# Scattering 80 instead of 72 edge columns one by one into a dense adjacency matrix

## The chip, the core and the metric

The kernel runs on one core of a Trainium2 chip. The metric is the device time of one execution in microseconds (us); lower is better. The core's engines are called as the profile calls them: PE (matmuls; PEld is its weight load), DVE (vector), ACT (activations), POOL (GpSimd, which here issues the indirect DMAs) and SP (which issues most of the plain DMAs).

## The reference, cut to what matters

One transformer layer: `x = x + attn(layernorm(x))`, then `x = x + ffn(layernorm(x))`, with x of shape (4, 1024, 256). The feed-forward part is a mixture of 8 experts, two for each token; it fills most of the time and isn't touched. In the attention part there is a sparse sum over a list of 32768 edges (row, column, value), and the change lies in how that sum is prepared:

```python
q = enc @ wq                                   # enc: attention output of batch 0 + dense
k = enc @ wk
scores = jnp.einsum('bid,bjd->bij', q, k) / jnp.sqrt(jnp.float32(WQK_DIM))
data = scores[0]                               # 1024 x 1024
contrib = adj_vals * data[adj_rows, adj_cols]
A_raw = jax.ops.segment_sum(contrib, adj_rows, num_segments=n)
alpha = jax.nn.softmax(A_raw)                  # one weight per row; used for every token
```

Rows and columns are drawn up to 2047 while n is 1024. An edge whose row is 1024 or more is dropped by the segment sum; a column of 1024 or more is clamped to 1023. So about a quarter of the edges have a row below 1024 and a column below 1023 (about 64 in each of 128 groups of 256 edges), and another quarter have the last column.

## The kernel before

**Edges.** The 32768 edges lie as 256 columns on 128 partitions. `edge_keys` (L203) marks the edges with a row below 1024 and a column below 1023 and makes three sort keys of each. `pick` (L251) takes the eight largest of each partition's keys with DVE's `max` and strikes them out; `picks` (L715) repeats that over groups of eight, so that after eleven groups the valid edges of a partition stand in order in `CC` = 88 packed columns. Edges of the last column go another way (`edge_last`, L368): one-hot tiles `ohl` on DVE and matmuls, 16 columns at a time, between the softmax work.

**A.** The sum becomes dense: A is a 1024 x 1024 matrix of edge values in DRAM, and `A_raw` comes from a matmul of A with k and a product with q. A exists as `PL` = 2 planes, `a_d[0]` and `a_d[1]`, zeroed at the start. `edge_pack` (L263) makes a cell number and a value for some of the packed columns with six small DVE operations, and `scatter` (L275) writes them: for each column one indirect DMA on POOL's queue, 128 single values, column i into plane i % 2. All 128 partitions take part; where a partition has no i-th valid edge, the cell number is out of bounds and nothing is written. Every eighth scatter (`REST` = 8) has an added dependence on the one before it.

**The rest.** Columns 0 to `CD` - 1 are scattered that way. The columns from `CD` to 87 hold few valid edges, and `edge_rest` (L291) puts these together into one column: it counts them (`full`, `nrest`), finds with a small matmul (L303) where each partition's rest begins, makes a one-hot tile `ohrest` of 128 x w on DVE (L310), with w = `CC - CD`, and moves the bytes of the edges with w small matmuls (L327) to `prest`. From there a handful of DVE operations make one cell and one value per partition, and column `CD` is scattered last (L342).

**Order of the work.** The groups of eight are picked in the steps `todo = {0: range(4, 6), 1: range(6, 9), 2: range(9, CC // 8)}` of the loop over the head pairs (L994), the earlier ones ahead of it; `picks` calls `edge_pack` for that part of its columns that lies below `CD`. The scheduler of the framework then orders each engine's instructions by dependences and priorities; each engine runs its own list in that order. On POOL's list the scatters stand one behind another, and each waits until the scatter eight places before it (on the same of eight completion semaphores) has landed.

**What needs A.** `counted` (L1071) reads both planes back, 1024 rows in eight steps c: `av` is the part of plane 0, `ac` that of plane 1, 512 KB each, read by SP's queue. DVE makes `nz` (which entries aren't zero, L1079) of each, PE sums these with sixteen tiny matmuls for each c (L1083), and DVE adds `ac` to `av` (L1086). There are three buffers for `nz` and two for `ac`. Plane counts are compared with the edge counts per row (`one_lo` and `one_hi` of `edge_hots`, L344, with the 88 small matmuls of L1110); a row in which two edges fell on one cell is `bad`, and its edges are done one by one (`direct`, L407). Between the scatters and this use PE has other work: the products `po` with the convolution band (L1047, L1057) and the q and k products `pqk` (L1093, L1095).

Of the kernel before, what the change touches and what calls it, by code (L numbers as in the profile page):

```python
# [11 lines left out]
ALU = mybir.AluOpType  # L12
# [4 lines left out]
P = 128  # L17
# [8 lines left out]
E = 32768  # L26
EC = E // P
CC = 88
CD = 72
EG = 8  # L30
DQ = 64
PL = 2
# [16 lines left out]
def tile_kernel(  # L49
# [137 lines left out]
    packed = [ed.tile([P, CC], F32, name=f"packed{i}") for i in range(3)]  # L187
    cell = ed.tile([P, CD + 1], I32, name="cell")
    pval = ed.tile([P, CD + 1], F32, name="pval")
    most = ed.tile([P, 1], F32, name="most")  # L190
# [84 lines left out]
    def scatter(cols):  # L275
        for i in cols:
            ins = nc.gpsimd.indirect_dma_start(  # L277
                out=a_d[i % PL],
                out_offset=bass.IndirectOffsetOnAxis(ap=cell[:, i : i + 1], axis=0),
                in_=pval[:, i : i + 1], in_offset=None,  # L280
                bounds_check=N * N - 1, oob_is_err=False,
            ).ins
            if i and i % REST == 0:
                tc.add_manual_dep(
                    ins, scattered[-1].name,
                    mybir.DependencyInfo(mybir.DependencyClass.Sync, mybir.DependencyReason.DATA),
                    reason="rest",
                )
            scattered.append(ins)

    def edge_rest(et, ps):  # L291


        w = CC - CD
        def some(name, dt=F32, w=w):
            return et.tile([P, w], dt, name=name, bufs=1)

        full, n, base = some("full"), some("nrest", w=1), some("base", w=1)
        first = packed[0][:, CD:]
        nc.vector.tensor_scalar(full, first, 0.0, None, ALU.not_equal)  # L300
        nc.vector.tensor_reduce(n, full, AX.X, ALU.add)
        pt = ps.tile([P, 512], F32, tag="ps", name="prest")
        mm(pt[:, 0:1], lhsT=low, rhs=n, start=True, stop=True)  # L303
        nc.vector.tensor_scalar(base, pt[:, 0:1], 512.0, None, ALU.add)
        to, tob = some("to"), some("tob", BF16)
        nc.vector.tensor_scalar(to, iota[:, 0:w], base, None, ALU.add)
        nc.vector.scalar_tensor_tensor(to, full, -512.0, to, ALU.mult, ALU.add)
        nc.vector.tensor_scalar(tob, to, 255.0, None, ALU.min)
        oh = et.tile([P, P, w], BF16, tag="ohl", name="ohrest")
        nc.vector.tensor_tensor(  # L310
            oh, tob.unsqueeze(1).to_broadcast([P, P, w]), iota_x, ALU.is_equal
        )

        bi = et.tile([P, 7, w], I32, name="restb", bufs=1)
        k = 0
        for s3, masks in zip(packed, ((255, 255, 15), (255, 255), (255, 255))):
            for j, mask in enumerate(masks):
                nc.vector.tensor_scalar(
                    bi[:, k], s3[:, CD:].bitcast(I32), 8 * j, mask,
                    ALU.logical_shift_right, ALU.bitwise_and,  # L320
                )
                k += 1
        by = et.tile([P, 8, w], BF16, name="rest8", bufs=1)
        nc.vector.tensor_copy(by[:, 0:7], bi)
        nc.vector.tensor_copy(by[:, 7], full)
        for i in range(w):
            mm(pt[:, 8:16], lhsT=oh[:, :, i], rhs=by[:, :, i], start=(i == 0), stop=(i == w - 1))  # L327
        r = some("restr", w=8)
        nc.vector.tensor_copy(r, pt[:, 8:16])
        c = some("restc", w=1)  # L330
        nc.vector.scalar_tensor_tensor(c, r[:, 1:2], 256.0, r[:, 0:1], ALU.mult, ALU.add)
        nc.vector.scalar_tensor_tensor(c, r[:, 2:3], 65536.0, c, ALU.mult, ALU.add)
        nc.vector.scalar_tensor_tensor(c, r[:, 7:8], -float(N * N), c, ALU.mult, ALU.add)
        nc.vector.tensor_scalar(cell[:, CD:], c, float(N * N), None, ALU.add)
        v2 = some("restv", I32, 2)
        rv = r[:, 3:7].rearrange("p (h l) -> p h l", l=2)
        nc.vector.scalar_tensor_tensor(v2, rv[:, :, 1], 256.0, rv[:, :, 0], ALU.mult, ALU.add)
        nc.vector.tensor_scalar(v2[:, 0:1], v2[:, 0:1], 16, None, ALU.logical_shift_left)
        nc.vector.tensor_tensor(
            pval[:, CD:].bitcast(I32), v2[:, 0:1], v2[:, 1:2], ALU.bitwise_or  # L340
        )
        scatter(range(CD, CD + 1))  # L342
# [110 lines left out]
    iota_x = ed.tile([P, P, 16], BF16, name="iota_x")  # L453
# [88 lines left out]
    with ExitStack() as at:  # L542
# [451 lines left out]
        for c in range(NP):  # L994
# [31 lines left out]
            if c in todo:  # L1026
                picks(todo[c])
                if todo[c].stop * 8 == CC:
                    edge_rest(hp, ps)
# [725 lines left out]
```

## Time and profile before

| | |
|---|---|
| Time, median of 5 runs | 1026.92 us (1024.29 to 1037.22) |
| Profiled execution: its own time | 1031.64 us |
| Profiled execution: span of its instructions | 1029.9 us |
| PE busy | 978.2 us, 95% of the span |
| DVE / ACT / POOL busy | 431.2 / 343.4 / 227.7 us |
| Scatters to A (L277) | 73, busy 78.3 us, from 41.3 to 177.9 us |
| First read of A (L1077) issued | 181.0 us |
| First count matmul on PE (L1083) | 204.7 us |
| Result of the count on DVE (L1121) | 226.8 us |

How to read it: the whole edge part lies in the first quarter of the span. The table's lower half gives the places of four events on the time axis of the profiled execution, counted from the start of the span. PE is busy almost everywhere, so a delay elsewhere shows in the time only where PE has to wait for it; and DVE, ACT and POOL have idle time in which work can be added. "Busy" for a scatter is the time that POOL spends on issuing it, not the time until the data is in DRAM.

### The profile page before, as it was taken

Reading aid. Unit: us, or ns where it says so; the run is one execution under the profiler, and the core shown is the slowest. Engines: PE = TensorE matmul, PEld = TensorE weight load, DVE = VectorE, ACT = ScalarE, POOL = GpSimd, SP = SyncE. Lnnn points to the kernel's source line nnn. Section 1 sums busy time; section 2 is a strip of 40 time slices with the busy share of each in tenths; the row PEclk is TensorE's granted clock in tenths of the full one; section 3 lists DMA queues with packets and bytes.
Section 4 is the critical chain, followed back from the end, with each engine's and each line's share of the span. In section 5 each row is a group of like instructions: output and inputs, shape, how many; then the busy total and the mean of one; then the engine's idle time right before and its main releaser. Section 6 shows DMA issues by size and latency. Waiting matters only on the chain. (4 is left out here: it accounts for less than half of the span.)

```text
span 1029.9 us, 13619 instructions
## 1 busy us (share of the span) xinstructions
PE 978.2 (95%) x5028; PEld 679.5 (66%) x5028; DVE 431.2 (42%) x1255; ACT 343.4 (33%) x653; POOL 227.7 (22%) x236
## 2 busy tenths in 40 slices
PE   4889998988998999999999999999999999999996
PEld 2668555564646465564656658888888888866664
DVE  7999188476764545525344211112121111222221
ACT  5345375230794836538262010110111101111111
POOL 0145665003011101001010112222323233222110
PEclk9999998979999999999999999999999999999998
DMA  9922100632501011010100324554556445678780
GB/s 339 310 60 84 42 2 2 225 115 12 185 22 62 1 62 42 21 41 22 62 21 21 128 69 147 205 192 149 172 201 220 174 158 191 204 292 307 275 303 13
DMA packets 77498, 132.65 MB, mean 129 GB/s; under 512 B 11981, under 2 KB 52302, under 8 KB 77424
## 3 DMA queue, kind: packets, MB, share of 16 engines
q1 hardware_dynamic: 66832, 115.85, 32.5%
q0 software_dynamic: 8848, 14.14, 4.7%
q10 hardware_dynamic: 1744, 1.70, 0.5%
q8 instruction: 43, 0.70, 0.3%
q14 instruction: 31, 0.25, 0.1%
HBM read 105.53 MB, written 26.80 MB: 128 GB/s over the span
## 5 line engine op out<-in xcount | busy, mean ns | idle before, releaser
L1493 PE MATMUL pa<-yT,w_a 128*128 128x512 f32 x256 | 124.7, 601 | 0.2 <-issue 0.2
L1493 PE MATMUL pb<-yT,w_a 128*128 128x512 f32 x256 | 121.7, 597 | 1.8 <-DVE h L1498 1.8
L1505 PE MATMUL po<-w_a,h 128*128 128x256 f32 x512 | 112.0, 379 | 0.0
L1505 PEld LDWEIGHTS po<-w_a,h 128*128 128x128 f32 x512 | 97.3, 190 | 17.0 <-issue 4.3
L1601 ACT ACTIVATE qs<-qa 128x512 f32<-128x512 f32 x52 | 31.0, 597 | 224.8 <-PE qa L1597 224.8
L1603 DVE TENSOR_TENSOR qh<-qs,qb 128x512 f32<-128x512 f32 x52 | 35.7, 687 | 162.0 <-PE qb L1597 162.0
L1597 PE MATMUL qa<-ypt,w_s 128*128 128x256 f32 x416 | 98.8, 380 | 0.4 <-issue 0.4
L1597 PE MATMUL qb<-ypt,w_s 128*128 128x256 f32 x416 | 98.3, 379 | 0.0
L1351 POOL DMA_INDIRECT meta_d<-info,pos x32 | 31.1, 972 | 286.1 <-DVE pos L1343 164.2
L1611 PE MATMUL qo<-w_s,qh 128*128 128x256 f32 x416 | 93.9, 379 | 0.0
L277 POOL DMA_INDIRECT a_d<-pval,cell x73 | 78.3, 1072 | 62.9 <-DMA a_d<-pval,cell 38.9
L1493 PEld LDWEIGHTS pb<-yT,w_a 128*128 128x128 f32 x256 | 48.4, 192 | 61.9 <-issue 57.7
L1597 PEld LDWEIGHTS qa<-ypt,w_s 128*128 128x128 f32 x416 | 78.1, 190 | 12.6 <-ACT ypt L147 1.1
L1597 PEld LDWEIGHTS qb<-ypt,w_s 128*128 128x128 f32 x416 | 79.1, 190 | 10.7
L1611 PEld LDWEIGHTS qo<-w_s,qh 128*128 128x128 f32 x416 | 78.1, 190 | 10.0
L1493 PEld LDWEIGHTS pa<-yT,w_a 128*128 128x128 f32 x256 | 46.8, 190 | 51.4 <-issue 49.9
L1573 POOL DMA_INDIRECT out<-ot,ids x36 | 36.1, 1004 | 195.3 <-DVE ot L1570 181.9
L1498 DVE TENSOR_TENSOR h<-sa,pb 128x512 f32<-128x512 f32 x64 | 43.6, 685 | 55.8 <-PE pb L1493 36.4
L1524 POOL DMA_INDIRECT ys<-y_d,ids x36 | 34.1, 947 | 131.0 <-PE pyp L1583 77.1
L1496 ACT ACTIVATE sa<-pa 128x512 f32<-128x512 f32 x64 | 38.1, 595 | 45.5 <-PE pa L1493 45.0
L1507 DVE SCALAR_TENSOR_TENSOR xa<-po,gates,xa 128x256 f32<-128x256 f32 x32 | 15.5, 483 | 80.8 <-PE po L1505 80.8
L1549 DVE TENSOR_TENSOR sh<-ssa,sb 128x512 f32<-128x512 f32 x20 | 13.7, 687 | 62.6 <-PE sb L1545 62.6
(476 smaller groups left out, 1401.3 us busy)
## 6 DMA issues: line engine op xcount, KB each, us to landing
w_s<-in_w_t SPq DMA_DIRECT2D x69, 1024.0 KB, 5.9
a_d<-zero SPq DMA_DIRECT2D x4, 2048.0 KB, 17.1
xa<-in_dense SPq DMA_DIRECT2D x4, 1024.0 KB, 13.6
av<-a_d SPq DMA_DIRECT2D x8, 512.0 KB, 6.2
ac<-a_d SPq DMA_DIRECT2D x8, 512.0 KB, 4.3
y_d<-enc SPq DMA_DIRECT2D x8, 512.0 KB, 3.2
e_d<-xa SPq DMA_DIRECT2D x8, 512.0 KB, 2.9
val_d<-fv SPq DMA_DIRECT2D x14, 256.0 KB, 2.0
```

The costliest lines, as they stand in the source:

```text
L277: ins = nc.gpsimd.indirect_dma_start(out=a_d[i % PL], out_offset=bass.IndirectOffsetOnAxis(ap=cell[:, i : i + 1], axis=0), in_=pval[:, i : ...
L1351: nc.gpsimd.indirect_dma_start(out=meta_d, out_offset=bass.IndirectOffsetOnAxis(ap=pos[:, b : b + 1], axis=0), in_=info[:, b, :], in_offse ...
L1493: mm(dst, lhsT=w[:, k, f * P : (f + 1) * P], rhs=rhs[:, k, :], start=(k == 0), stop=(k == KD - 1))
L1496: nc.scalar.activation(sa, pa, AF.Silu)
L1498: nc.vector.tensor_tensor(ht, sa, pb, ALU.mult)
L1505: mm(po, lhsT=hs[f][:, b * P : (b + 1) * P], rhs=w2[:, f, :], start=(f == 0), stop=(f == NF - 1))
L1524: nc.gpsimd.indirect_dma_start(out=ys, out_offset=None, in_=src, in_offset=bass.IndirectOffsetOnAxis(ap=ids[:, 0, s : s + 1], axis=0),)
L1573: nc.gpsimd.indirect_dma_start(out=out_rows, out_offset=bass.IndirectOffsetOnAxis(ap=ids[:, 1, s : s + 1], axis=0), in_=ot, in_offset=None ...
L1597: mm(dst[:, i, :], lhsT=wt[:, k, f * P : (f + 1) * P], rhs=yst[:, k].rearrange("p i n -> p (i n)"), start=(k == 0), stop=(k == KD - 1))
L1601: nc.scalar.activation(sa, pa, AF.Silu)
L1603: nc.vector.tensor_tensor(h, sa, pb, ALU.mult)
L1611: mm(po, lhsT=hs[f // 2][:, f % 2, i * P : (i + 1) * P], rhs=w2[:, f, :], start=(f == 0), stop=(f == NF - 1))
```

## The change

`CD` goes from 72 to 80. Nine groups of eight columns become ten that are packed and scattered column by column (81 scatters with the last, where there were 73), and `edge_rest` handles 8 columns instead of 16. Since `ohrest` is now 128 x 8, the comparison's other operand is cut to the first 8 of the 16 repeats of `iota_x`.

```diff
@@ -26,7 +26,7 @@
 E = 32768
 EC = E // P
 CC = 88
-CD = 72
+CD = 80
 EG = 8
 DQ = 64
 PL = 2
@@ -308,7 +308,7 @@
         nc.vector.tensor_scalar(tob, to, 255.0, None, ALU.min)
         oh = et.tile([P, P, w], BF16, tag="ohl", name="ohrest")
         nc.vector.tensor_tensor(
-            oh, tob.unsqueeze(1).to_broadcast([P, P, w]), iota_x, ALU.is_equal
+            oh, tob.unsqueeze(1).to_broadcast([P, P, w]), iota_x[:, :, 0:w], ALU.is_equal
         )
```

In the step `range(9, 11)`, where before only `edge_rest` ran, `edge_pack` now packs columns 72 to 79 first and queues their eight scatters; the scatter of the rest, now column 80, stands behind them and is again a multiple of `REST`.

## The prediction

> **What bounds the kernel now.** I read the page's list of costliest groups first, then the timelines of POOL, SP, PE and DVE between 160 and 230 us, and last the table of busy times by stretch. In the list, the scatters:
>
> ```profile
> L277 POOL DMA_INDIRECT a_d<-pval,cell x73 | 78.3, 1072 | 62.9 <-DMA a_d<-pval,cell 38.9
> ```
>
> POOL is busy for 78.3 us of the 136.6 between the first scatter (41.3) and the end of the last (177.9), and most of its idle time is waiting for earlier scatters to land. The last groups of eight were picked on DVE by 98 us, so since then POOL alone has been late: a backlog, not a lack of input. Its end, in the timeline of POOL (start, duration, instruction, idle time before it):
>
> ```profile
> 163.69 0.97 POOL L277 DMA_INDIRECT a_d<-pval,cell  x1 [1.88 <-DMA a_d<-pval,cell]
> 164.97 0.97 POOL L277 DMA_INDIRECT a_d<-pval,cell  x1 [0.30 <-issue]
> 167.18 0.97 POOL L277 DMA_INDIRECT a_d<-pval,cell  x1 [1.25 <-DMA a_d<-pval,cell]
> ...
> 173.59 1.43 POOL L277 DMA_INDIRECT a_d<-pval,cell  x1 [0.30 <-issue]
> 176.92 0.97 POOL L277 DMA_INDIRECT a_d<-pval,cell  x1 [1.90 <-DVE ohl L374]
> 233.47 0.35 POOL L1164 PARTITION_ALL_REDUCE worst<-nbad  x1 [55.58 <-DVE taken L1168]
> ```
>
> The last one's wait is put down to DVE, but its cell was written at 173.0; it is the landing of the scatter before it, 1.9 us after that one's end, as for all "rest" scatters. Behind the last scatter POOL has nothing until 233.5. SP's reads of A follow, and PE's timeline shows who waits for them:
>
> ```profile
> 180.98 0.32 SPq L1077 DMA_DIRECT2D av<-a_d  x1
> ...
> 190.22 0.32 SPq L1077 DMA_DIRECT2D ac<-a_d  x1
> 190.58 3.26 SPq L1077 DMA_DIRECT2D av<-a_d  x4
> 205.76 16.08 SPq L1077 DMA_DIRECT2D ac<-a_d  x5
> ```
>
> ```profile
> 201.23 3.60 PE L1095 MATMUL pqk<-a1T,wox 128*128 128x512 f32 x8
> 204.66 0.54 PE L1083 MATMUL cnt<-onesb,nz 128*128 128x1 bf16 x16
> ...
> 212.14 3.57 PE L1110 MATMUL cnt<-one_hi,one_lo 128*64 128x16 bf16 x88
> 215.97 1.02 PE L1116 MATMUL pe<-edges,spread 64*128 64x8 f32 x4 [0.26 <-ACT edges L1113]
> 216.92 0.80 PE L1083 MATMUL cnt<-onesb,nz 128*128 128x1 bf16 x24
> ```
>
> The reader is to see that PE runs without a gap from 180.7 to 215.7 on work that needs nothing of A, and takes the first count at 204.66, though DVE had it ready at 189. From 217 on the order is turned round: DVE and the reads set the pace.
>
> ```profile
> 205.04 0.69 DVE L1079 TENSOR_SCALAR nz<-ac 128x1024 bf16<-128x1024 f32 x1 [5.29 <-PE cnt L1083]
> 217.33 0.69 DVE L1079 TENSOR_SCALAR nz<-ac 128x1024 bf16<-128x1024 f32 x1 [3.02 <-PE cnt L1083]
> 222.46 0.69 DVE L1079 TENSOR_SCALAR nz<-ac 128x1024 bf16<-128x1024 f32 x1 [0.36 <-DMA ac<-a_d]
> 226.76 0.16 DVE L1121 TENSOR_TENSOR less<-less,cnt 128x8 f32<-128x8 f32 x1
> ```
>
> L1121 at 226.76 releases the rest (PE waits 1.16 us for `bad`), and from there nearly all is PE. So what moves L1121 moves the end, one for one; what doesn't, costs nothing.
>
> **The change, part by part.**
>
> *Removed on PE and DVE.* Eight of the sixteen L327 matmuls go: the sixteen take 1.17 us (168.66 to 169.83), so 0.59 less. `ohrest` has 1024 elements instead of 2048 and now reads 8 of 16 neighbours; the nearest row with such runs of eight is `one_hi` (L362, 1408 elements in 0.88 us), which gives 0.64 instead of 1.17: 0.53 less. If it ran like `one_lo` (1408 in 1.43) it would be 1.04, only 0.13 less. Both lie on a path, since DVE runs from 166 to 176 nearly without a gap and waits 0.66 us for `prest` (L329). In the changed program's order L374's next `ohl` stands ahead of L329 and of the scaling of `a` (L981), so that wait is filled too. I get `ohl` 13 at 170.05 instead of 171.22. PE's `pt` (L986) comes 0.2 us later through the swap, and the granted clock is 0.50 there (165 to 170: 0.98), so not all of it survives. `po` at 180.72 comes 0 to 1.2 us earlier; I take 0.7.
>
> *Added on DVE.* Six pack operations for columns 72 to 79, near 97 us. The pack of 24 columns took 0.16 to 0.18 each, 1.03 in sum. They are hidden: right behind, DVE waits 0.23 and 1.49 us for PE's `pfv`, and PE is busy without a gap from 80 to 120. Without that cover, 1.0 us.
>
> *Added on POOL.* Eight scatters, all ahead of the last. With "rest" waits at every eighth the price of eight is read from the starts of numbers 24, 32, 40, 48, 56, 64, 72: 94.79, 107.64, 119.47, 133.21, 148.09, 163.69, 176.92, steps of 12.85, 11.83, 13.74, 14.88, 15.60, 13.23. The longest were beside DVE's `ohl` run, where single scatters took up to 2.03 instead of 0.97. From 177 on DVE does little of that, so I take 13.0 (range 11.8 to 15.6). Scatter 80 then starts at 189.9 and ends at 190.9. Before, the first read came 3.09 us after the last scatter's end (180.98 - 177.89); so now at 194.0, 13.0 later. Behind the waiting scatter POOL has nothing, and SP only the reads.
>
> *What the 13 us meet.* Between 181 and 191 the six first reads moved 3.1 MB, and between 191 and 199 five more 2.6 MB: 1.55 us per read, the first landing 3.6 after its issue. From 194.0: av0 197.6, ac0 199.1, av1 200.7, ac1 202.2, av2 203.8, av3 205.3. DVE has both `nz` of c = 0 by 199.8; PE wants them at 204.66 (204.0 if 0.7 is gained): over 4 us of cover. The third `ac` waits for the first sum at 201.0, then av4 to av7; they land from 206.9 to 213.1, and DVE wants that `ac` at 210.7: covered. The fourth `ac` waits as before for PE's first count, but lands behind av7 at 214.6, where DVE had it at 211.89: 2.7 late. That pushes its `nz` to 215.3, the sum to 216.4, the next `nz` to 217.0. PE wants these in its 24 counts from 216.92, whose last eight start at 217.1. So the cover ends almost exactly here. The fifth `ac` is there at 216.1, the sixth is issued at 216.5 and lands 3.3 later, 219.8, where DVE wants it at 219.68. The write of k (0.26 MB, issued 212.65) falls among these reads: 0.26 / 350 GB/s is another 0.7. The remaining `ac`s are tied to DVE's own pace as before.
>
> *Sum.* The 0.7 gained ahead is swallowed by this chain, which now ends last; what is left is 0.1 + 0.7 - 0.3 of cover = +0.5 us at L1121. Bounds: scatters at 11.8 and the DVE gain let through, -1.0; scatters at 15.6 put the first read at 196.6, +2.4; reads at 1.7 instead of 1.55 us add 12 x 0.15 = 1.8.
>
> On the profiled execution this is 1031.64 + 0.5; that run was 4.7 us above the median of the five, so on their scale 1026.92 + 0.5 = 1027.4.
>
> A rule speaks against the change: the Trainium skill, SBUF — State Buffer, section "A bandwidth-pool intuition that's wrong", says that a GpSimd DMA which takes some 0.62 us alone took about 3.1 us beside a DVE operation holding the port that both share. This trace shows 0.97 growing to 2.03 at most. By the page eight scatters would be an estimated 25 us; by the rows they are 13.
>
> **The rivals.**
>
> 1. *The backlog comes out on PE: slower.* Place: POOL from 177 on; price: the eight scatters take as long as the first eight did, 66.78 - 41.29 = 25.5 us. The first read is then at 206.5. It decides once that read is later than about 194.3, and from there costs one for one: +12.2, 1039. For it: those eight waited 3 to 4.7 us for landings, and scatters beside DVE work took up to 2.03 us instead of 0.97. Against it: from 36 to 60 the DMA engines were busy 0.70 of the time, from 165 to 181 0.01 to 0.02. Chance 0.14.
> 2. *The tail is paid in part.* Scatters at 15.6 and slower reads, 2.4 + 1.8: +4, 1031. For it: the cover ends within half a microsecond of my value. Chance 0.17.
> 3. *The gain ahead comes through.* L310 and L327 give 1.1 us and the reads are early enough (193, if 180.98 was set by `xbd`, ended 180.67, and not by the landing): -1.1, 1025.8. Chance 0.11.
> 4. That the change doesn't do what it says: the changed program has 81 scatters and 8 matmuls at L327, and all other lists keep their order. No chance of its own.
>
> **How the numbers follow.** My forecast, within 2 us of before, has 0.58: 1027.4. The five runs spread over 12.9 us, so a measurement of this kernel can tell about 1% from no change; a median of such runs carries some 3 us of its own. The range goes from the third case less this (1022.5) to the second plus it, and some way toward the first: 1036. The likeliest case's own range is 1024 to 1031. Slower by over 1% is the first rival, 0.14; faster by over 1% has no mechanism here, 0.03 for the spread; the rest 0.83.
>
> **What would show it.** Right: 81 scatters, the last starting near 190; the first read near 194; PE without a gap from 180 to 215; the count at 204 without a wait on DVE; DVE waiting for `ac` near 212 to 215; L1121 within 1 us of 226.8. Wrong: PE waiting at L1083 ahead of 211, the first read after 197, or L310 not shorter than 1.1.

## The result, and the profile after

The changed kernel takes 1032.66 us (median of 52 runs, 1025.46 to 1038.25); the kernel before, run beside it, takes 1029.2 us (median of 94 runs, 1024.29 to 1037.22). The ratio is 1.003 with a 95% interval of 1.0021 to 1.0039: by the ratio 3.1 us more, surely more than nothing, and a third of the 1% that the prediction set as its bound for a difference. The profiled execution took 1032.75 us (span 1030.8), 1.1 more than that of before.

First the scatters, in the page's list of costliest groups, and the end of POOL's row of them in the timeline (start, duration, instruction, idle time before it and what ended it):

```profile
L277 POOL DMA_INDIRECT a_d<-pval,cell x81 | 88.0, 1087 | 69.3 <-DMA a_d<-pval,cell 36.6
```

```profile
161.66 0.97 POOL L277 DMA_INDIRECT a_d<-pval,cell  x1 [1.88 <-DMA a_d<-pval,cell]
...
170.22 1.98 POOL L277 DMA_INDIRECT a_d<-pval,cell  x1 [0.30 <-issue]
172.50 1.97 POOL L277 DMA_INDIRECT a_d<-pval,cell  x1 [0.30 <-issue]
174.77 0.97 POOL L277 DMA_INDIRECT a_d<-pval,cell  x1 [0.30 <-issue]
178.46 0.97 POOL L277 DMA_INDIRECT a_d<-pval,cell  x1 [2.72 <-DVE lo L351]
...
187.81 0.97 POOL L277 DMA_INDIRECT a_d<-pval,cell  x1 [0.30 <-issue]
190.67 0.97 POOL L277 DMA_INDIRECT a_d<-pval,cell  x1 [1.89 <-DMA a_d<-pval,cell]
```

Number 64 is at 161.66, number 72 at 178.46 and the last one at 190.67. The added eight took 12.21 us (178.46 to 190.67). The eight ahead of them took 16.80 instead of 13.23, mainly because two of them, beside DVE's `ohl` work, lasted nearly 2 us each and the wait behind them was longer. In DVE's timeline stand the two comparisons during which they were issued:

```profile
170.14 1.22 DVE L374 TENSOR_TENSOR ohl<-row_lo_x,iotab 128x2048 bf16<-128x2048 bf16 x1
...
172.41 1.22 DVE L374 TENSOR_TENSOR ohl<-row_lo_x,iotab 128x2048 bf16<-128x2048 bf16 x1
```

They end at 171.36 and 173.63, and each of the two scatters ends 0.84 us behind (172.20 and 174.47). So it is with every scatter over 1.3 us in the two profiles, 10 before and 11 after: it ends 0.83 to 0.85 us behind the end of a DVE operation. How long a scatter takes depends on where in such an operation it is issued. POOL's row now reaches nearly 14 us (to 191.64) into the stretch in which PE works on `po`. SP's reads of A follow in its timeline:

```profile
192.91 0.32 SPq L1077 DMA_DIRECT2D av<-a_d  x1
...
199.62 0.32 SPq L1077 DMA_DIRECT2D ac<-a_d  x1
199.98 2.15 SPq L1077 DMA_DIRECT2D av<-a_d  x4
203.43 17.34 SPq L1077 DMA_DIRECT2D ac<-a_d  x5
```

The first one waits for the last scatter to land. The DMA view of a window that holds only this scatter gives its time from issue to landing (last number, us), before (window 176.5 to 177.9):

```profile
a_d<-pval,cell POOLq DMA_INDIRECT x1, 3.9
```

and after (190.5 to 191.6):

```profile
a_d<-pval,cell POOLq DMA_INDIRECT x1, 2.1
```

So it landed at 180.8 before and at 192.8 after, and the read followed 0.1 to 0.2 us later in both.

PE's timeline shows that most of the delay met work that needed nothing of A:

```profile
177.70 1.13 PE L1047 MATMUL po<-a1T,xbd 128*128 128x512 f32 x2 [0.93 <-DVE xbd L1039]
...
201.64 0.54 PE L1083 MATMUL cnt<-onesb,nz 128*128 128x1 bf16 x16
...
209.12 3.85 PE L1110 MATMUL cnt<-one_hi,one_lo 128*64 128x16 bf16 x88
213.23 1.02 PE L1116 MATMUL pe<-edges,spread 64*128 64x8 f32 x4 [0.26 <-ACT edges L1113]
214.18 1.04 PE L1083 MATMUL cnt<-onesb,nz 128*128 128x1 bf16 x24
```

There is no bracket between 177.70 and 213.23: PE took the first count at 201.64 without a wait, 23.94 us behind L1047, exactly as before (180.72 to 204.66). In DVE's timeline the delay does come out, behind that:

```profile
196.48 0.69 DVE L1079 TENSOR_SCALAR nz<-av 128x1024 bf16<-128x1024 f32 x1 [11.58 <-DMA av<-a_d]
...
212.35 0.69 DVE L1079 TENSOR_SCALAR nz<-ac 128x1024 bf16<-128x1024 f32 x1 [3.40 <-DMA ac<-a_d]
...
218.61 0.69 DVE L1079 TENSOR_SCALAR nz<-ac 128x1024 bf16<-128x1024 f32 x1 [1.48 <-DMA ac<-a_d]
...
223.78 0.69 DVE L1079 TENSOR_SCALAR nz<-ac 128x1024 bf16<-128x1024 f32 x1 [0.41 <-DMA ac<-a_d]
...
225.64 0.16 DVE L1121 TENSOR_TENSOR less<-less,cnt 128x8 f32<-128x8 f32 x1
```

The 11.58 us at the first `av` cost nothing, since PE didn't ask for that count yet. The 3.40 at the fourth `ac` and the 1.48 at the sixth are in the chain: before, the fourth had no wait at all, as its row in DVE's timeline of the kernel before shows:

```profile
211.89 0.69 DVE L1079 TENSOR_SCALAR nz<-ac 128x1024 bf16<-128x1024 f32 x1
```

Counted from L1047, the fourth comes 3.48 us later than before (34.65 instead of 31.17). Most of that is still covered: the fifth, for which DVE had to wait for PE before, comes only 0.39 later (37.00 instead of 36.61). The sixth comes 1.95 later (40.91 instead of 38.96), because its read waits for a buffer that the late fourth holds (issued 36.51 us behind L1047 instead of 33.02). That delay reaches L1121. L1121 stands at 225.64, earlier than before in absolute time only because this execution was already 2.02 us earlier at L303 (162.84 instead of 164.86), which lies ahead of what the change touches at the end. Measured from mark to mark, the two spans differ by:

| Stretch | Before, us | After, us | Difference |
|---|---|---|---|
| start of the span to L303 (count of the rest's edges) | 164.86 | 162.84 | -2.02 |
| L303 to the first `po` (L1047) | 15.86 | 14.86 | -1.00 |
| L1047 to L1121 | 46.04 | 47.94 | +1.90 |
| L1121 to the first load of `w_a` (L1294) | 30.99 | 31.10 | +0.11 |
| that load to the end | 772.15 | 774.06 | +1.91 |

So in this pair the edge stage (second and third line) pays 0.9 us, and the rest of the difference is not there. The last line has 1.69 of its 1.91 us in one group, the 52 `px` matmuls behind L1262, with equal work in both. Before, in PE's timeline:

```profile
259.24 11.47 PE L1229 MATMUL px<-wo,a1T 128*128 128x256 f32 x52
```

and after:

```profile
258.24 13.16 PE L1229 MATMUL px<-wo,a1T 128*128 128x256 f32 x52
```

By the table of busy times by stretch, the granted clock was 0.90 from 240 to 257 us and 1.00 from 257 to 271 in the kernel before; in the changed one it was 1.00 and 0.88. So a slow stretch stands ahead of these matmuls in one execution and within them in the other. This doesn't follow the kernel: on chip 14 and chip 5 (below) the changed kernel has 11.47 too, and on chip 5 a variant of the kernel before has 13.16.

### The profile page after: what moved, and what is told of

It reads as the page before. It is cut to its first block, busy times and chain, and to the rows that moved or that the text cites. A ratio compares the mean times of both kernels' runs of the same rounds, so it can differ in the third digit from the quotient of the medians.

```text
span 1030.8 us, 13626 instructions
## 1 busy us (share of the span) xinstructions
PE 979.0 (95%) x5020; PEld 679.9 (66%) x5020; DVE 431.8 (42%) x1261; ACT 343.4 (33%) x653; POOL 238.1 (23%) x244
## 5 line engine op out<-in xcount | busy, mean ns | idle before, releaser
L1493 PE MATMUL pb<-yT,w_a 128*128 128x512 f32 x256 | 124.0, 606 | 2.5 <-DVE h L1498 2.5
L277 POOL DMA_INDIRECT a_d<-pval,cell x81 | 88.0, 1087 | 69.3 <-DMA a_d<-pval,cell 36.6
```

The costliest lines, as they stand in the source:

```text
L277: ins = nc.gpsimd.indirect_dma_start(out=a_d[i % PL], out_offset=bass.IndirectOffsetOnAxis(ap=cell[:, i : i + 1], axis=0), in_=pval[:, i : ...
L1493: mm(dst, lhsT=w[:, k, f * P : (f + 1) * P], rhs=rhs[:, k, :], start=(k == 0), stop=(k == KD - 1))
```

## The experiments

Theory A, late reads: the added scatters make the reads of A late; about 13.5 us of that lie behind PE's `po` and `pqk` work, and past it the delay comes out one for one at L1121. Against it stands that the 3 us come from another part than the late reads; each expectation says what its rivals would give. Times are compared with the kernel before on the same chip. Three chips were met: on chip 9 the kernel before took 1030.57 us, much as in the comparison above; on chips 14 and 5 it took 1059.67 and 1058.55. The changed kernel as it is was not run on chip 9, only its parts and variants.

### More or fewer scatters ahead of the last

The kernel before, with the eight (or sixteen) last packed columns scattered a second time to the same cells, ahead of the scatter of the rest. The values are the same, so only the time on POOL and the DMAs are added; `edge_rest` keeps its 16 columns.

```diff
+        scatter(range(CD - 8, CD))      # sixteen: range(CD - 16, CD)
         scatter(range(CD, CD + 1))
```

These were run first on chip 14.

> Only the eight added scatters: the kernel before, with columns 64 to 71 scattered a second time (same cells, same values) ahead of the last. Theory A: first read near 194 us, ratio 1.003 to 1.005, more than the whole change costs, since nothing is given back. Theory B: the scatters are covered, ratio 1.000.

Measured: 1.002 (0.9975 to 1.0064).

> The dose doubled: columns 56 to 71 are scattered a second time ahead of the last. Theory A: the first read comes near 207 us, PE waits at its first count, and what is past the cover's end counts one for one: 13 us more than with eight, ratio 1.012 to 1.019. Theory B: POOL's queue isn't on the path; ratio at most 1.003.

Measured: 1.0102 (1.0046 to 1.0159). This is no answer to the question, though it looks like one: on that chip the last scatter (207.36 to 209.06) ends ahead of L1047 (214.44), and L1047 to L1121 took 45.19 us, so no read came late. In this execution L303 to L1047 took 19.96 us, where the kernel before took 15.86 in its profile; what the 1% consists of isn't shown. On chip 9 the same kernels could be read.

> Only the eight added scatters (columns 64 to 71 a second time). Theory A: how late the first read is against L1047 decides. Up to 13.3 us behind it, L1047 to L1121 takes 46 us; past that, the rest counts one for one. Where the backlog of POOL is as in the first profile, the read comes 13 to 14 us behind L1047 and the ratio is 1.000 to 1.003; where other stages ran longer, 1.000. Theory B: 1.000 anywhere.

Measured: 1.0021 (1.0000 to 1.0042), median 1031.78 us. The first read came 14.78 us behind L1047, and L1047 to L1121 took 47.31.

> Sixteen added scatters (columns 56 to 71 a second time). Theory A: where POOL's backlog is as in the first profile, the first read comes 26 to 28 us behind L1047, PE waits at its first count, L1047 to L1121 takes 59 to 61 us, ratio 1.012 to 1.016. Theory B: L1047 to L1121 stays at 46 to 48, ratio at most 1.003.

Measured: 1.0146 (1.0116 to 1.0177), median 1046.07 us. The first read came 26.72 us behind L1047, and L1047 to L1121 took 58.85. PE's timeline of this run (lines here are one higher than in the kernel before, so L1084 is the count) has the wait that the changed kernel just avoids:

```profile
199.26 3.60 PE L1096 MATMUL pqk<-a1T,wox 128*128 128x512 f32 x8
209.86 0.37 PE L1084 MATMUL cnt<-onesb,nz 128*128 128x1 bf16 x8 [7.00 <-DVE nz L1080]
```

From eight to sixteen the reads are 11.94 us later and the stretch is 11.54 us longer: 0.97 to one. That is theory A's slope; with the points below it also gives the threshold. The delay comes out in more than one place: the first count is 31.11 us behind L1047 instead of 23.94, 7.2 of the 12.8 us by which the stretch is longer than before, and the rest comes behind it.

### The narrower `edge_rest` alone

The kernel before, with `edge_rest` handling columns 72 to 79 only; nothing is added to POOL.

```diff
-        w = CC - CD
+        w = 8
-        first = packed[0][:, CD:]
+        first = packed[0][:, CD : CD + w]
...
-            oh, tob.unsqueeze(1).to_broadcast([P, P, w]), iota_x, ALU.is_equal
+            oh, tob.unsqueeze(1).to_broadcast([P, P, w]), iota_x[:, :, 0:w], ALU.is_equal
...
-                    bi[:, k], s3[:, CD:].bitcast(I32), 8 * j, mask,
+                    bi[:, k], s3[:, CD : CD + w].bitcast(I32), 8 * j, mask,
```

> Only the narrower rest: 8 columns (72 to 79) are put together, 73 scatters as before; the few edges of columns 80 to 87 are not scattered, so that their rows are counted as bad and done one by one. Theory A: the time from L303 to L1047 falls from 15.9 to about 14.9 us, the first read stays near 181 us, ratio 0.999 (-1 us). Theory B: the narrower rest or the swapped order of DVE is itself what costs; ratio 1.002 to 1.004.

Measured on chip 14: 1.5677 (1.5593 to 1.5760), far from every expectation, and a fault of the experiment. The edges left out all sit in one partition; the counts of their rows and of A no longer agree, so more than `EG` of that partition's edges became `bad`, and the long way for that case ran, about 600 us. It says nothing on the question. The second form sets the limit of that test so that the long way isn't taken:

```diff
-        nc.vector.tensor_scalar(worst, worst, float(EG), 0.0, ALU.subtract, ALU.max)
+        nc.vector.tensor_scalar(worst, worst, 64.0, 0.0, ALU.subtract, ALU.max)
```

> Only the narrower rest: columns 72 to 79 are put together, 73 scatters as before. The six edges of columns 80 to 87 are left out of A, and the limit above which bad rows take the long way is lifted, so that this doesn't start. Theory A (late reads): the time from L303 to the first convolution product (L1047) is about 1 us shorter than with 16 columns, the first read comes at most 1 us after L1047 starts, from L1047 to L1121 46 us; ratio 0.998 to 0.999. Theory B (not the scatters): the narrower rest or DVE's swapped order costs by itself, ratio 1.002 to 1.004.

Measured on chip 9: 1.0021 (1.0000 to 1.0041), median 1032.61 us. L303 to L1047 took 15.07 us where the kernel before took 15.86, so the stage ahead does get shorter; L1047 to L1121 took 45.14. In its profiled execution the edge stage is 1.7 us shorter than before, and yet the median is 2 us longer. Here theory A alone missed: with no read late enough to cost anything, a slowdown of about the same size is there, though its interval begins at nothing. (The profiled execution itself took 1030.99, below the median of its kernel.) The first read missed its expectation too: it came 9.27 us behind L1047, not at most 1, though no scatter was added. Part of that is the last scatter, in POOL's timeline:

```profile
182.74 4.41 POOL L277 DMA_INDIRECT a_d<-pval,cell  x1 [1.90 <-DMA a_d<-pval,cell]
```

It lasted 4.41 us instead of 0.97, to 187.15, which is again 0.84 us behind the end of a run of DVE's comparisons (L356 and L362, 181.38 to 186.31). And it started 18.64 us behind L303, where it had been 12.06 in the kernel before: the narrower rest alone moves POOL's row by several us. The `px` matmuls of this run, in PE's timeline, stand as in the changed kernel:

```profile
256.67 13.16 PE L1229 MATMUL px<-wo,a1T 128*128 128x256 f32 x52
```

### The changed kernel without the waits for every eighth scatter

```diff
-REST = 8
+REST = 1000
```

> The changed kernel without the wait of every eighth scatter for the one ahead of it (REST 1000). 81 scatters, but some 16 us of POOL's waits gone. Theory A: the last scatter goes out right after its cell is written (near 171 us), the reads start with L1047 or ahead of it, L1047 to L1121 takes 46 us, and the 1 us gained by the narrower rest is seen: ratio 0.998 to 1.000, against 1.003 with the waits. Theory B: nothing changes against the changed kernel, 1.003.

Measured on chip 9: 1.0017 (0.9994 to 1.0040), median 1032.18 us. All 81 scatters are issued by 178.49 us (171 was expected for the last), where the changed kernel needed until 191.64, and the first read comes 1.13 us behind L1047. L1047 to L1121 took 46.62, 1.3 less than after. In DVE's timeline the third `ac` waits for PE, as before, and the fourth (at 211.29) has no wait for a transfer:

```profile
210.08 0.69 DVE L1079 TENSOR_SCALAR nz<-ac 128x1024 bf16<-128x1024 f32 x1 [3.08 <-PE cnt L1083]
...
211.29 0.68 DVE L1079 TENSOR_SCALAR nz<-ac 128x1024 bf16<-128x1024 f32 x1
```

So the late reads are taken away and the stretch behaves as theory A says. But L303 to L1047 took 15.51 us, so of the 1 us expected from the narrower rest this execution shows only 0.35; and the interval of the time takes in both that of before and 1.003, so it doesn't decide between the theories. In this run the `px` matmuls took 11.47 us, so they are not the place of the difference every time.

### The points together

All on chips where the reads can be late, one profiled execution each:

| Kernel | First read behind L1047, us | L1047 to L1121, us |
|---|---|---|
| before | 0.26 | 46.04 |
| after, no waits for every eighth | 1.13 | 46.62 |
| before, narrow `edge_rest` | 9.27 | 45.14 |
| before, eight scattered twice | 14.78 | 47.31 |
| after | 15.21 | 47.94 |
| before, sixteen scattered twice | 26.72 | 58.85 |

Up to 9.27 us a later read costs nothing (the three values spread over 1.5 us); from 14.78 on it costs one for one. Drawn back one for one from the last point to the mean of the first three (45.9), the line bends at 26.72 - 12.9 = 13.8 us (with the slope of 0.97, at 13.4). The changed kernel lies 1.4 to 1.8 us beyond it. With the spread of the first three the bend is known to about 1 us, an estimate.

### The same two kernels on the other chips

The changed kernel as it is, on chip 14 and on chip 5.

> The changed kernel once more, for a second profile beside the others on one chip. Theory A (late reads): the eight added scatters put the first read of A some 12 us later, past the cover that PE's own work gives; the time from PE's first convolution product (L1047) to L1121 grows from 46.0 us to about 48, and the narrower rest gives about 1 us back ahead of it. Ratio near 1.003. Theory B (not the scatters): the time from L1047 to L1121 is again near 46, and the 3 us appear elsewhere, behind 257 us or ahead of L303.

Measured on chip 14: 0.9996 (0.9951 to 1.0041). Its table of waits between 40 and 200 us (us in total, times, longest) has rows of a kind that the first profile of the kernel before doesn't have in that part, among them:

```profile
ACT ft L842 <- remote: 17.1, 3, 8.1
...
DVE zw L911 <- remote: 9.6, 2, 7.3
```

"remote" is the profile's word for a release that nothing on this core gave. Five such rows, on ACT and DVE, come to 37.8 us, and in this execution L303 comes at 199.75 us instead of 162.84. That these waits are the delay is likely but not shown, since waits of two engines can lie side by side; nor is it shown what they wait for. With L303 so late, POOL has caught up: its last scatter, which waited 22.78 us for its `cell`, was over ahead of L1047, and L1047 to L1121 took 46.18. With the reads hidden, the changed kernel costs nothing here that can be told; the interval leaves room for 4 us.

> The changed kernel on one chip with the next three. Theory A (late reads): first read 14 to 16 us behind L1047, L1047 to L1121 47 to 48 us, ratio 1.002 to 1.004. Theory C (the clock): the runs of the changed kernel carry a lower mean granted clock than those of before (0.978 to 0.979 against 0.980 to 0.981), and at one and the same clock the two differ by 1 to 1.5 us only.

Measured on chip 5: 1.0074 (1.0033 to 1.0115). The reads are hidden here as well (1.38 us ahead of L1047, L1047 to L1121 46.63), so these 8 us can't be late reads. They are not explained: the waits for "remote" differ from run to run by several us, and one profile of each kernel doesn't tell a difference of kernels from that.

> The kernel before without the waits of every eighth scatter. The control to the same edit of the changed kernel: before, the reads have 13 us of cover already, so Theory A expects no gain, ratio 0.999 to 1.001, with the first read within 1 us of L1047. If this too is 2 us slower, an earlier end of the scatters isn't worth anything and the 2 us of the other variants come from where the clock falls, not from an edit.

The edit is `REST = 1000` in the kernel before. Measured on chip 5: 1.0371 (1.0307 to 1.0434), far from the expected 1.000, though the first read came ahead of L1047 and L1047 to L1121 took 46.21. So the run doesn't serve as the control that it was meant to be. On chip 9 the same edit, in the changed kernel, cost nothing that can be told. Its table of waits between 36 and 240 us:

```profile
ACT ft L842 <- remote: 29.5, 2, 19.8
DVE zw L911 <- remote: 23.2, 2, 13.3
...
DVE fv L858 <- remote: 18.6, 3, 10.1
```

The "remote" waits have grown, and L303 comes at 227.51 us. That the waits for every eighth scatter shield other transfers from POOL's on such a chip fits this, but is argued only.

### The fourth `ac` on another queue

It lands late because it stands behind four `av` reads on SP's queue (issued 203.43, in use at 212.35). So the `ac` reads were given to POOL's queue, in the changed kernel and in the kernel before.

```diff
-                    nc.sync.dma_start(out=ac, in_=a_v[i][:, c])
+                    (nc.gpsimd if i else nc.sync).dma_start(out=ac, in_=a_v[i][:, c])
```

> The changed kernel with the reads of plane 1 (`ac`) issued by POOL instead of SP, so that the fourth isn't queued behind av4 to av7. Scatters and first read as in the changed kernel. Theory A, with the fourth ac as the place: L1047 to L1121 goes back from 48 to 46 us, ratio 0.999 to 1.002 and some 2 us below the changed kernel. If L1047 to L1121 stays at 48, the queue behind av7 wasn't what was late.

> The kernel before with the reads of plane 1 issued by POOL. Before, PE and not the reads set the pace up to 217 us, so Theory A expects no more than 0.5 us from the last few reads: ratio 0.999 to 1.001. If it is faster than that, the tail from 217 to 227 us was bound by SP's queue in the kernel before too, and this version beats both.

Measured on chip 5: 1.0122 (1.0057 to 1.0187) and 0.9977 (0.9935 to 1.0019). The reads were hidden on this chip in either kernel, so nothing was there to be gained; L1047 to L1121 took 47.29 and 47.60, up to 1 us more than the 46.63 of the changed kernel from SP's queue. The question is left open, and no version surely beat the kernel before.

## Why the prediction was right, and where it wasn't

Forecast: no change that can be told, from a late transfer which PE's other work covers almost exactly. The measured 1032.66 us lies in the range, and the change is 0.3%; that much held, and so did the mechanism. The size didn't: +3.1 us where +0.5 was forecast. The time forecast was 1027.4 and the likeliest case's own range ended at 1031, so 1032.66 lies beyond it; 2.3 of the 5.3 us are the base alone, since the kernel before took 1029.2 us in the comparison and 1026.92 in the five runs that the sum started from.

*The cover.* The prediction put its end at a first read of 194.3 us, with L1047 at 180.0: 14.3 behind it. The runs bend near 13.4 to 13.8, and then follow one for one (0.97). This was the step that decided between "same" and the first rival, and it held; with eight scatters more the first rival is what was measured (1.0146, with PE waiting 7.00 us).

*The scatters and the first read.* Two terms were off and nearly cancelled. The added eight took 12.21 us (13.0 forecast), but the group ahead of them grew by 3.57 (16.80 instead of 13.23), which the sum had at nothing: measured from L303, the last scatter came 15.8 us later, not 13.0. On the other side, the prediction took the 3.09 us from the last scatter's end to the first read as the time of a landing. It was that of one slow landing: the last scatter before took 3.9 us from issue to landing, while the median of the eight scatters issued between 165 and 181 us was 2.1, and the last one of the changed kernel took 2.1. The gap from its end to the first read is 1.27 us (191.64 to 192.91), and 1.27 as well in the runs with eight and with sixteen. The third rival's reason, that `xbd` and not the landing had let the first read go, doesn't hold: on chip 5 the changed kernel's first read goes out at 205.53, ahead of `xbd` (206.43). The read came at 192.91 (194.0 forecast), 15.21 behind L1047 (14.0 forecast). That the two errors nearly cancel in the time of the read was luck.

*The gain ahead.* L310 takes 0.69 us (0.64 forecast, 1.17 before), the eight matmuls of L327 0.66 (1.17 the sixteen before), and L1047 is 1.00 us earlier against L303 (0.7 forecast). The third rival had asked that this gain come through; it didn't.

*The tail.* The fourth `ac` came in use 34.65 us behind L1047 (34.6 forecast) and DVE waited for it as said, at 212.35. The term that was mis-sized is the sixth `ac`: issued 36.51 us behind L1047 (36.5 forecast), it was in use 4.40 us later, where the sum had 3.3 and 0.7 for the write of k, and DVE waited 1.48 us. The sixth `ac` of the kernel before shows this already: issued at 213.74 beside the same write, it took 4.3 to land. And the 0.3 of cover that the sum subtracts at the end wasn't there. In sum the stretch from L1047 on grew by 1.90 (1.2 forecast, the 0.7 gained and the 0.5 left), and the edge stage by 0.9 net instead of 0.5. The second rival, "the tail is paid in part", has the size of the time that was measured (+4), but not its place: it wanted 4 us of late reads, and there are 1.9, less the 1.0 gained.

*What had no term.* The other 2 us. Something of that size is measured in all three of the small variants on chip 9, also in the one with 1.7 us less in its edge stage (1.0021) and the one without late reads (1.0017), though each interval reaches down to about nothing. A part of them goes with the granted clock: among the runs of the changed kernel a mean clock lower by 0.001 goes with 0.68 us more, and on chip 9 the mean clock was 0.9806 for the kernel before and 0.9784, 0.9788 and 0.9794 for the narrow, the eight-twice and the no-wait variant. With 0.64 us for each 0.001, the slope over the runs of that chip, that is 0.7 to 1.4 us; at equal clock the three stay 0.7 to 1.1 us above the kernel before, each with a standard error of about 0.55, so that none of them is surely above it. The `px` group shows one way in which a lower clock costs time. The reverse is there too: the run with sixteen, whose PE waits, has a mean clock of 0.9735, so a lower mean can come from lost time as well as cause it. Why a shorter or later edge stage should meet the lower clock more often was not settled, nor what the last microsecond is: the theory of late reads, less the gain ahead, explains 0.9 of the 3.1 us and no experiment places the rest. The cause of these 2 us stays open.

A page bears on this. The Trainium skill, TensorE: Matmul & The Clock Gate, section "Part 1: The HAM clock gate (the "warmup" mystery)", says that the array drops to half its clock after a window of about 3.4 us without enough work, and that these windows run free of the program. This case agrees in so far as equal work took 11.47 or 13.16 us, and the slow stretch stood in another place; that the windows' phase decides it, no run here shows.

The rule that the prediction set against the change, from the Trainium skill, SBUF — State Buffer ("A bandwidth-pool intuition that's wrong"), would have made eight scatters an estimated 25 us. They took 12.21 in the changed kernel, and none of its scatters took over 2.04 us. The page puts the time down to a wait until DVE's operation ends, and in that this case agrees with it: the long scatters ended 0.83 to 0.85 us behind the end of a DVE operation, and the one of 4.41 us in the run with the narrow `edge_rest` ended so behind a whole run of them. The operations here were shorter (1.22 us for an `ohl`), and few of the scatters met one.

## What to carry to other kernels

When work is added to a queue that is late, find the first instruction that needs its result and the work that the needing engine has in hand until then: that cover is a length in us, and the cost is the delay less the cover, which here held to about a microsecond. A landing time read from one transfer can be an outlier (here 3.9 us, where its neighbours had a median of 2.1), so take it from several before moving a gap along. And where the expected change is a few tenths of a percent, leave room for what no term of the sum contains: here three variants, with late reads and without, all measured 1 to 2 us above the kernel before, and the cause stayed open.

## What the runs showed of the hardware

- Time and granted clock go together: 0.64 to 0.68 us for each 0.001 of its mean over the span. The same 52 matmuls took 11.47 us at a clock of 1.00 and 13.16 at about 0.88.
- A wait for the earlier scatters at every eighth costs POOL some 13 us over the whole row (last scatter at 177.52 us without it, 190.67 with it), and that cost stayed off the end nearly in full.
- A scatter that was issued during a long DVE comparison was held until 0.84 us behind its end: the changed kernel's at 170.22 and 172.50 lasted 1.98 and 1.97 us instead of 0.97, and the last one of the narrow run 4.41.
- The last scatter's landing took 3.9 us before and 2.1 after, with equal work; the first read of A followed within 0.2 us.
- Equal programs took 1030.6 us on one chip and 1059 on two others; in the profiles of the latter "remote" waits stand ahead of L303. On such a chip the removal of the waits for every eighth scatter cost the kernel before 3.7%, where on the quieter one it cost the changed kernel nothing that could be told. An experiment on a late queue has to be run where that queue is late.
